# A two-block residual convolution network on one Trainium2 core: SBUF-to-SBUF transfers of the mixed stage sent by quarters, two for each unit of products

## The chip, the cores and the metric

The kernel runs on one core of one Trainium2 chip. The core has a matrix engine (TensorE; PE in the profile, its weight loads PEld), a vector engine (DVE), a scalar engine (ACT), GpSimd (POOL) and SyncE (SP), which here only issues transfers. Each engine works through its own instructions in order and waits on semaphores for the others. Every transfer that is issued from SP stands in SP's queue in program order: one that has to wait, or takes long to issue, holds up those behind it.

The metric is the device time of one execution in microseconds (us), lower is better. All data is float32.

## The reference

Two bottleneck blocks of a residual network, one after the other, on x of shape (64, 1024, 14, 14). Batch statistics are taken over all 64 images, so every normalization needs the whole convolution before it.

```python
def _bn(x, gamma, beta):
    mean = jnp.mean(x, axis=(0, 2, 3), keepdims=True)
    var = jnp.var(x, axis=(0, 2, 3), keepdims=True)
    ...
out = relu(_bn(_conv(x, w1, b1, 1, 0), g1, be1))     # 1x1, 1024 -> 256
out = relu(_bn(_conv(out, w2, b2, 1, 1), g2, be2))   # 3x3, 256 -> 256
out = _bn(_conv(out, w3, b3, 1, 0), g3, be3)         # 1x1, 256 -> 1024
out = softplus(residual_scale)[0] * out
out = relu(x + out)
```

## The kernel before

The 64 images are 32 tiles of two images, 392 pixels each (`T` = 32, `PX` = 392). Channels lie on the 128 partitions: 256 channels are two slots `s`, 1024 channels are eight slots `o`. The output of the second convolution of all images, `y_all`, stays on chip: 128 x 2 x 12544.

Block 0 runs as first convolution, second convolution, the **mixed stage** (`mixed`), and the **fused stage** (`fused`), which does the rest of block 0 together with the first convolution of block 1. Block 1 then has its own second convolution, a stage for statistics, and the final one.

**The mixed stage** needs the mean and variance of the third convolution over all images before that convolution can be normalized. It gets them in two ways at once:

- *The second half of the images* (tiles 16 to 31) is multiplied by w3 at once, and the raw result z is written out to be picked up later. Tile 16 goes first, in `first()` (L1522 to L1544 or so), as eight plain convolutions `conv3`, one for each output slot, with banks of the matrix engine's memory named cy, cx, cp, ay, ap, ax. Tiles 17 to 31 go through `direct_stream` (L605 and on): 60 **units**, four to a tile, each with two output slots and seven half-size products instead of eight (class `Direct`). A unit is cut into seven steps (0 to 6); the caller gets control after every step. Steps 0, 2, 3 and 4 are the products p1, p5, p2 and p6 of this unit, steps 1, 5 and 6 the products p7, p4 and p3 of the unit before. `after1` (ACT) copies bank cy to cx, on which p2 then adds; `after7` is L591 and `after3` is L597, both on DVE. Each unit writes its result to `kept[:, q]`, one of four slots, q = unit mod 4. The first write is that of p5 in step 2. When p3 of the unit is done, L599 sends the slot to z from SP's queue. The same slot is written again four units later, and that write has to wait until the transfer has landed.
- *The first half* (tiles 0 to 15, 6272 pixels) needs only the sums over pixels of y times y transposed (the gram matrix, `gram_products`). It is cut in five **pieces** (`MOVES`: four of 1280 pixels, one of 1152). Each piece is normalized on ACT (`norm_piece`, eight instructions of a quarter of the piece and one slot s), has a constant taken off on DVE (`less`, L1457; "centred"), is sent from `y_all` to a `home` by sixteen SBUF-to-SBUF transfers on SP's queue (`move`, L1493: four partition blocks i to four places j; i also picks a quarter of the pixels), and then transposed by DVE in chunks of 128 pixels, two at a time (`turn`, L1251). Two homes take turns: piece k needs the transposes of piece k - 2 to be done. Four chunks are a batch of gram products on the matrix engine; there are thirteen batches, at units 9, 12, ... 45 (`at`), fed by the generator `batches()`: the products of a batch at step 2, the transposes at step 3 of that unit and of the next.

The loop at the end of `mixed` lays all of this beside the units by hand: one normalization for each unit (`norms`, step 1), centrings at step 3, `moves = {9: 1, 17: 2, 25: 3, 33: 4}` (all sixteen transfers of piece 1 at unit 9, and so on). Piece 0 is normalized inside `first()`, two instructions behind each of the plain convolutions 3 to 6; its centring and its sixteen transfers follow `first()`. The order of matrix-engine, ACT and most other instructions is kept as it stands in the program (`keep_in_program_order`, `pinned`).

**The fused stage** reads z back in rows of 392 (tile p, slot o), eight for each of the tiles 16 to 31. A row is scaled and added to x, with DVE (L1828) for even o and with POOL (`by_pool`: L1814 multiplies, L1815 adds) for odd o. The POOL instructions of the first tile's four odd rows are put in front of the loop; for those rows the loop then only goes on with what follows. On POOL they stand ahead of the additions L537 and L542 of the stage's own products. ACT's relu behind L542 stands in ACT's order ahead of `au` (`after1` of `Conv1`), which the products `ay<-at,ws` of the matrix engine wait for.

Of the kernel before, what the change touches and what calls it, by code (L numbers as in the profile page):

```python
# [18 lines left out]
CS = C // P  # L19
MS = M // P  # L20
# [6 lines left out]
CH = 2  # L27
NZT = 6

Q = P // 2  # L30
# [8 lines left out]
NGRAM = KEPT * PX  # L39
MOVES = 5 * P * CH, 5 * P * CH, 5 * P * CH, 5 * P * CH, 9 * P  # L40
BATCH = 4
# [28 lines left out]
def bottlenecks(ctx: ExitStack, tc: tile.TileContext, x, w1s, w2s, w3s, pars, out):  # L70
# [6 lines left out]
    y_all = keep.tile([P, MS, NPX], FP, tag="y", name="y")  # L77
# [1363 lines left out]
    def mixed(psum, pool, one, x_right, x_left, aff, minus_c, w3, made_c, summed_c, summed_a, mv3, xs, coming_x):  # L1441
# [14 lines left out]
        def less(y, s, eng=nc.vector):  # L1456
            tc.keep_in_program_order(eng.tensor_scalar(y, y, minus_c[:, s : s + 1], None, ALU.add))  # L1457
# [3 lines left out]
        def norm_piece(k):  # L1461

            a, e = pieces[k]
            for s in range(MS):
                for i in range(4):
                    h = (e - a) // 4
                    norm(s, y_all[:, s, a + i * h : a + i * h + h], aff, act)
                    normed[k] += 1
                    yield

        def home(k):
            a, e = pieces[k]
            x = homes[k % 2][:, : MS * (e - a)].rearrange("p (s j f) -> p s j f", s=MS, j=4)
            return x, a, (e - a) // 4

        centered = collections.Counter()

        def center():

            k = next((k for k in range(len(pieces)) if centered[k] < MS * 2), None)  # L1480
            if k is not None and normed[k] >= 2 * centered[k] + 2:
                s, i = divmod(centered[k], 2)
                a, e = pieces[k]
                h = (e - a) // 4 * 2
                less(y_all[:, s, a + i * h : a + i * h + h if i == 0 else e], s)
                centered[k] += 1

        def move(k):
            assert centered[k] == MS * 2 and (k < 2 or k - 2 in turned)
            x, a, run = home(k)  # L1490
            for i, j in itertools.product(range(4), range(4)):
                tc.keep_in_program_order(
                    nc.sync.dma_start(  # L1493
                        out=x[32 * i : 32 * i + 32, :, j],
                        in_=y_all[32 * j : 32 * j + 32, :, a + i * run : a + i * run + run],
                    )
                )

        def blocks(t):
            return [[two(t, s)[:, i * H // 2 : (i + 1) * H // 2] for i in range(2)] for s in range(MS)]  # L1500
# [2 lines left out]
        ready = {}  # L1503
# [20 lines left out]
        def first():  # L1524


            t = KEPT
            norm(0, two(t, 0), aff, act)
            normed_less(two(t, 1), 1, nc.vector)
            less(two(t, 0), 0)  # L1530
            tags = "cy", "cy", "cx", "cp", "ay", "ay", "ap", "ax"
            for i, (q, row) in enumerate(itertools.product(range(CS // 2), range(2))):
                z, o = kept[:, q, row], q + row * CS // 2
                ps = conv3(psum, t, o, w3, tags[i])
                act(z, ps, AF.Copy)
                nc.vector.bn_stats(own[:, o, 0, :], ps)
                if row:
                    put(t, q)
                if i == 0:
                    for _ in itertools.chain(summed_c, prepare(t + 1), itertools.islice(coming[t + 2], MS)):  # L1540
                        pass
                if 2 < i < 7:
                    next(norms)
                    next(norms)  # L1544

        def put(t, q):
            to = zs[t - KEPT].rearrange("p (s f) -> p s f", s=CS)[:, q :: CS // 2, :]
# [11 lines left out]
        def chunks():  # L1559

            for k, (a, e) in enumerate(pieces):
                x, count = home(k)[0], (e - a) // P
                for i in range(0, count, CH):
                    zt = next(zts)
                    turn(zt, x, i, min(CH, count - i))
                    if i + CH >= count:
                        turned.add(k)
                    for c in range(min(CH, count - i)):
                        yield zt[:, c], (k, i + c)

        def batches():
            queue, total = chunks(), NGRAM // P
            bounds = [*range(0, total, BATCH), total]
            ready = [list(itertools.islice(queue, BATCH))]
            yield
            for a, e in zip(bounds, bounds[1:]):
                for i, (v, _) in zip(range(a, e), ready.pop()):
                    gram_products(upper, lower, v, i == 0, i == total - 1, True)
                yield
                ready.append([])  # L1580
                for _ in range(BATCH // CH):
                    ready[0].extend(itertools.islice(queue, CH))
                    yield

        norms = itertools.chain.from_iterable(norm_piece(k) for k in range(len(pieces)))
        coming = {t: prepare(t) for t in range(KEPT + 1, T)}
        first()
        both = psum.tile(512, "ap")
        upper, lower = both[:, : 3 * Q + 1], both[:, 3 * Q + 1 : 5 * Q + 3]
        zts, by, gs = gram_tiles(pool, NGRAM, 3)  # L1590
        for _ in range(2 * MS):
            center()
        move(0)
        tail, grams = None, iter(())
        moves = {9: 1, 17: 2, 25: 3, 33: 4}
        at = list(range(9, 48, 3))
        at_first, _ = beds((None, None))
        made, done = [], []

        def make(*tags):  # L1600
            for tag in tags:
# [12 lines left out]
        def finish():  # L1614
            aggregated(3)
            make("cy", "cp")

        pinned.append(True)
        for unit, step in direct_stream(units(), between, finish):
            t, q = KEPT + 1 + unit // 4, unit % 4  # L1620
            if step == 1 and unit > 0:
                next(norms, None)
            if step == 3 and unit == at[0] - 1:
                grams = batches()
                next(grams)
            if step == 2 and unit in at or step == 3 and (unit in at or unit - 1 in at):
                next(grams, None)
            if step == 3:
                if q < 2 and t + 1 < T:
                    next(coming[t + 1], None)  # L1630
                if len(moves) > len(done):
                    center()
                if unit in moves:
                    done.append(unit)
                    move(moves[unit])
                if unit in (20, 23, 26, 29):
                    next(summed_a)
                if unit in (44, 48):
                    coming_x()
                if 50 <= unit < 50 + AHEAD:  # L1640
                    bring(at_first[unit - 50], unit - 50)
                if unit == 57:
                    assert next(tail, "end") == "end"
                    for half in range(2):
                        to = gram_entry[:, :, 3 * half : 3 * half + 3]
                        nc.gpsimd.memset(to[:, :, 0], NGRAM / 2)
                        run(nc.vector.tensor_copy(to[:, :, 1], mv3[:, :, 0]))
                        run(nc.vector.tensor_scalar(to[:, :, 2], mv3[:, :, 1], NGRAM / 2, None, ALU.mult))
            if step == 5 and q == 1 and t + 1 < T:
                next(coming[t + 1], None)  # L1650
            if step == 5 and unit == 57:
                column_sums(pool, blocks(positions()[2]), n, eng=nc.gpsimd, to=ahead())
            if unit == 59 and step in (3, 5):
                aggregated(step // 4)
            if step == 6 and unit > at[-1] + 1 and (tail is None or unit < 57):
                if tail is None:
                    assert next(grams, "end") == "end"
                    tail = conv3_stats(
                        psum, pool, (upper, lower, by, gs), w3, mv3, ("ax", "ap", "ax", "ap"), homes[1], ("ax", "ax", "ap")
                    )  # L1660
                next(tail, None)
# [116 lines left out]
    def fused(psum, pool, one, right, coming, xs, raw, w1, w3, aff, par, stats, border, begun):  # L1778
# [26 lines left out]
        def kept_rows():  # L1805
# [8 lines left out]
                run(nc.gpsimd.tensor_scalar(z, z, scale[:, o : o + 1], None, ALU.mult))  # L1814
                run(nc.gpsimd.tensor_add(v, v, z))  # L1815

            for o in range(1, CS, 2):
                by_pool(*row(o, 1, o), o)
            for r, (p, o) in enumerate(itertools.product(range(1, T, 2), range(CS))):
                while r == len(at) and later:  # L1820
                    later.pop(0)()
                    yield
                v, z = row(r, p, o)
                if o % 2:
                    if p > 1:
                        by_pool(v, z, o)
                else:
                    run(nc.vector.scalar_tensor_tensor(v, z, scale[:, o : o + 1], v, ALU.mult, ALU.add))  # L1828
                for q in behind[r]:
                    bring(at[q], q)  # L1830
                later.append(partial(rest, v, p, o))
                if len(later) > 2:
                    later.pop(0)()
                yield
# [365 lines left out]
```

## Time and profile before

| | us |
|---|---|
| median of 3 runs | 1922.06 |
| lowest, highest | 1920.35, 1925.96 |
| the profiled execution, its own time | 1926.02 |
| its span | 1924.2 |
| its mean granted clock of TensorE | 0.995 |

The span is the time from the first to the last instruction in the trace of that one execution. A row of a timeline gives start, duration (both in us from the span's start), engine and line, what is written and read, how many instructions are merged in it, and in brackets how long the engine idled before it and what ended that. "SPq" is SP's queue; the duration there is that of the issue, not of the transfer. In a table of DMA issues the last number is the median time from issue to landing. A row of a table of windows gives the window, its length, the busy time of each engine with the number of its instructions, the granted clock of TensorE (1.00 is full speed), the mean busy share of the DMA engines and GB/s.

### The profile page before, as it was taken

How to read it: one execution, taken by the hardware profiler on the slowest of the kernel's cores; microseconds unless marked ns; L12 is line 12 of the kernel's file. 1: busy time of each engine (PE TensorE's matmuls, PEld its weight loads, DVE VectorE, ACT ScalarE, POOL GpSimd, SP SyncE). 2: the span in 40 equal slices, each digit the busy share in tenths (PEclk: the TensorE clock that was granted, in tenths of full speed). 3: DMA queues.
4: the chain of work that ended last, by engine and by line, in shares of the span. 5: the costliest groups of instructions: out<-in, count | busy, mean ns of one | idle time of the engine just before them, and what ended most of it. 6: DMA issues, size and time to landing. Idle time of an engine off the chain costs nothing. (4 is left out here: it accounts for less than half of the span.)

```text
span 1924.2 us, 28592 instructions
## 1 busy us (share of the span) xinstructions
PE 1889.5 (98%) x9778; PEld 1569.0 (82%) x9778; DVE 1573.1 (82%) x2464; ACT 1087.6 (57%) x2275; POOL 748.5 (39%) x764
## 2 busy tenths in 40 slices
PE   9999999999998999999999999999999999999999
PEld 5555557999996788889999999989999987555555
DVE  5787767999996666778878787789999987888886
ACT  2222214676775554465555555456777782666666
POOL 0111100211206535277676777602112041776665
PEclk9999999999999999999999999999999999999999
DMA  7777644887953535678787789648879457799997
GB/s 286 274 249 260 221 163 146 208 220 209 219 186 127 170 130 176 215 286 287 293 297 284 277 308 276 240 159 214 218 208 223 156 151 282 253 348 342 346 347 271
DMA packets 262370, 458.20 MB, mean 238 GB/s; under 512 B 59152, under 2 KB 228976, under 8 KB 249040
## 3 DMA queue, kind: packets, MB, share of 16 engines
q1 hardware_dynamic: 225248, 374.88, 58.2%
q0 software_dynamic: 31216, 28.81, 7.6%
q10 hardware_dynamic: 5760, 52.67, 6.8%
q8 instruction: 78, 1.28, 0.3%
q14 instruction: 68, 0.56, 0.1%
HBM read 289.44 MB, written 141.03 MB: 224 GB/s over the span
## 5 line engine op out<-in xcount | busy, mean ns | idle before, releaser
L332 ACT ACTIVATE x<-x,shift 128x392 f32<-128x392 f32 x452 | 260.0, 614 | 78.2 <-DVE x L514 31.4
L159 PE MATMUL columns<-v,ub 128*128 128x224 f32 (+1 forms) x1536 | 302.5, 338 | 1.3 <-ACT columns L332 0.8
L159 PEld LDWEIGHTS columns<-v,ub 128*128 128x128 f32 x1536 | 268.7, 188 | 7.5 <-ACT columns L332 1.5
L332 ACT ACTIVATE cu<-cy,scale 128x196 f32<-128x196 f32 (+1 forms) x360 | 175.5, 500 | 168.8 <-PE cy L159 161.2
L159 PE MATMUL ay<-at,ws 128*128 128x196 f32 (+1 forms) x768 | 193.2, 383 | 3.4 <-ACT au L332 2.1
L159 PEld LDWEIGHTS ay<-at,ws 128*128 128x128 f32 x768 | 136.3, 190 | 38.8 <-ACT au L332 2.4
L514 DVE SCALAR_TENSOR_TENSOR x<-cp,scale,x 128x196 f32<-128x196 f32 (+1 forms) x240 | 124.6, 519 | 46.7 <-PE cp L159 45.2
L641 POOL TENSOR_TENSOR x<-x,cu 128x392 f32<-128x392 f32 x120 | 125.5, 1047 | 73.2 <-DVE x L514 72.4
L332 ACT ACTIVATE au<-ay 128x196 f32<-128x196 f32 (+1 forms) x140 | 53.8, 384 | 173.1 <-PE ay L159 158.9
L159 PE MATMUL l<-diffs,ub 128*128 128x224 f32 (+1 forms) x768 | 149.6, 337 | 0.3 <-ACT sd L1921 0.3
L159 PE MATMUL m<-sums,ua 128*128 128x224 f32 (+1 forms) x752 | 146.0, 336 | 0.2 <-DVE sums L757 0.2
L159 PEld LDWEIGHTS l<-diffs,ub 128*128 128x128 f32 x768 | 134.6, 189 | 1.2 <-ACT sd L1921 0.6
L159 PEld LDWEIGHTS m<-sums,ua 128*128 128x128 f32 x752 | 131.4, 189 | 1.4 <-DVE sums L757 0.8
L159 PE MATMUL cx<-y,w 128*128 128x196 f32 (+1 forms) x396 | 126.1, 404 | 0.8 <-POOL y L1522 0.8
L537 POOL TENSOR_TENSOR x<-x,cu 128x196 f32<-128x196 f32 (+1 forms) x120 | 104.8, 873 | 48.6 <-ACT cu L332 27.8
L1055 POOL DMA_DIRECT2D y<-f x24 | 32.7, 1687 | 232.4 <-DVE f L975 232.4
L159 PE MATMUL cy<-y,w 128*128 128x196 f32 (+1 forms) x372 | 117.3, 403 | 0.7 <-DVE y L1457 0.7
L542 POOL TENSOR_TENSOR x<-x,cu 128x392 f32<-128x392 f32 x60 | 79.5, 1325 | 87.2 <-DVE x L514 83.0
L332 ACT ACTIVATE y<-y,shift,scale 128x1568 f32<-128x1568 f32 (+7 forms) x94 | 106.7, 1154 | 6.6 <-DVE shift L1953 6.5
L206 POOL DMA_DIRECT2D u<-y x48 | 26.0, 543 | 213.2 <-ACT y L332 212.4
L159 PE MATMUL cy<-ct,wt 128*128 128x196 f32 x384 | 96.4, 333 | 10.9 <-ACT cu L332 10.8
L936 ACT ACTIVATE columns<-m 128x448 f32<-128x448 f32 (+1 forms) x144 | 70.9, 492 | 58.9 <-PE m L159 54.0
(303 smaller groups left out, 4560.2 us busy)
## 6 DMA issues: line engine op xcount, KB each, us to landing
ub<-u SPq DMA_DIRECT2D x92, 768.0 KB, 5.5
x<-in_x SPq DMA_DIRECT2D x35, 1568.0 KB, 8.5
mid<-x ACTq DMA_DIRECT2D x32, 1568.0 KB, 8.1
x<-mid SPq DMA_DIRECT2D x32, 1568.0 KB, 8.7
out<-x SPq DMA_DIRECT2D x123, 392.0 KB, 7.0
x<-in_x SPq DMA_DIRECT2D x108, 392.0 KB, 7.8
z<-kept SPq DMA_DIRECT2D x64, 392.0 KB, 3.0
ua<-u SPq DMA_DIRECT2D x92, 256.0 KB, 3.1
```

What stands on the lines that cost most here:

```text
L159: tc.keep_in_program_order(nc.tensor.matmul(*args, **kw))
L206: nc.gpsimd.dma_start(out=us[b][i][:, s, o], in_=u)
L332: tc.keep_in_program_order(nc.scalar.activation(*args, **kw))
L514: run(nc.vector.scalar_tensor_tensor(v, bank, self.scale[:, o : o + 1], v, ALU.mult, ALU.add))
L537: run(nc.gpsimd.tensor_add(self.part(1, 1), self.part(1, 1), u3))
L542: run(nc.gpsimd.tensor_add(v, v, self.u12))
L641: nc.gpsimd.tensor_add(v, v, self.u12[:, i * self.n : (i + 1) * self.n])
L936: copy(v, m, AF.Copy)
L1055: nc.gpsimd.dma_start(out=out_rows[3][:, o], in_=fa[:, o, :full], accum_op=ALU.add)
```

## The change

In the mixed stage:

- A piece is normalized quarter by quarter (both slots s of a quarter, then the next), where it was slot by slot.
- A quarter is centred by two instructions of 320 (288 in the last piece) columns, one for each slot, where it was half a piece of one slot by one instruction. At units 2, 4, ... 32 one quarter each.
- The four transfers of a quarter can be sent as soon as that quarter is centred. Piece 0 is centred and sent quarter by quarter in `first()`, behind the plain convolutions 3 to 6. Pieces 1 to 4 are sent by two transfers a unit, in units 3 to 10, 13 to 20, 20 to 27 and 28 to 35.
- The first three steps of unit 0 are put in front of the last plain convolution of `first()`.
- The first two transposes, both at unit 8 before, are made at units 7 and 8.

In the fused stage the POOL instructions of the fourth odd row (row 7) go from in front of the loop to that row's place in the loop.

```diff
         def norm_piece(k):
             a, e = pieces[k]
-            for s in range(MS):
-                for i in range(4):
+            for i in range(4):
+                for s in range(MS):
                     h = (e - a) // 4
                     norm(s, y_all[:, s, a + i * h : a + i * h + h], aff, act)
...
-        def center():
-            k = next((k for k in range(len(pieces)) if centered[k] < MS * 2), None)
-            if k is not None and normed[k] >= 2 * centered[k] + 2:
-                s, i = divmod(centered[k], 2)
-                a, e = pieces[k]
-                h = (e - a) // 4 * 2
-                less(y_all[:, s, a + i * h : a + i * h + h if i == 0 else e], s)
-                centered[k] += 1
-
-        def move(k):
-            assert centered[k] == MS * 2 and (k < 2 or k - 2 in turned)
-            x, a, run = home(k)
-            for i, j in itertools.product(range(4), range(4)):
+        def center(k, i):
+            assert normed[k] >= MS * i + MS
+            for s in range(MS):
+                less(y_all[:, s, quarter(k, i)], s)
+
+        def move(k, i, places):
+            assert normed[k] >= MS * i + MS and (k < 2 or k - 2 in turned)
+            for j in places:
                 tc.keep_in_program_order(
                     nc.sync.dma_start(
-                        out=x[32 * i : 32 * i + 32, :, j],
-                        in_=y_all[32 * j : 32 * j + 32, :, a + i * run : a + i * run + run],
+                        out=home(k)[0][32 * i : 32 * i + 32, :, j], in_=y_all[32 * j : 32 * j + 32, :, quarter(k, i)]
                     )
                 )
...
             for i, (q, row) in enumerate(itertools.product(range(CS // 2), range(2))):
                 z, o = kept[:, q, row], q + row * CS // 2
+                if i == 7:
+                    for _ in itertools.islice(stream, 3):
+                        pass
                 ps = conv3(psum, t, o, w3, tags[i])
...
                 if 2 < i < 7:
                     next(norms)
                     next(norms)
+                    center(0, i - 3)
+                    move(0, i - 3, range(4))
...
-            ready = [list(itertools.islice(queue, BATCH))]
-            yield
+            ready = [[]]
+            for _ in range(BATCH // CH):
+                ready[0].extend(itertools.islice(queue, CH))
+                yield
...
-        for _ in range(2 * MS):
-            center()
-        move(0)
...
-        moves = {9: 1, 17: 2, 25: 3, 33: 4}
+        moves = {}
+        for k, begin in enumerate((3, 13, 20, 28), 1):
+            for i in range(8):
+                moves[begin + i] = moves.get(begin + i, ()) + ((k, i // 2, (i % 2 * 2, i % 2 * 2 + 1)),)
...
-            if step == 3 and unit == at[0] - 1:
-                grams = batches()
+            if step == 3 and at[0] - 3 < unit < at[0]:
+                grams = batches() if unit == at[0] - 2 else grams
                 next(grams)
...
-                if len(moves) > len(done):
-                    center()
-                if unit in moves:
-                    done.append(unit)
-                    move(moves[unit])
+                if 0 < unit <= 32 and unit % 2 == 0:
+                    center((unit - 1) // 8 + 1, (unit - 1) % 8 // 2)
+                for where in moves.get(unit, ()):
+                    move(*where)
...
-            for o in range(1, CS, 2):
+            for o in 1, 3, 5:
                 by_pool(*row(o, 1, o), o)
...
                 if o % 2:
-                    if p > 1:
+                    if p > 1 or o == CS - 1:
                         by_pool(v, z, o)
```

More of the change, by code (lines that the diff above doesn't have):

```diff
@@ L1474, in home, with quarter @@
             return x, a, (e - a) // 4
-        centered = collections.Counter()
-        def center():
-            k = next((k for k in range(len(pieces)) if centered[k] < MS * 2), None)
-            if k is not None and normed[k] >= 2 * centered[k] + 2:
-                s, i = divmod(centered[k], 2)
-                a, e = pieces[k]
-                h = (e - a) // 4 * 2
-                less(y_all[:, s, a + i * h : a + i * h + h if i == 0 else e], s)
-                centered[k] += 1
-        def move(k):
-            assert centered[k] == MS * 2 and (k < 2 or k - 2 in turned)
-            x, a, run = home(k)
-            for i, j in itertools.product(range(4), range(4)):
+        def quarter(k, i):
+            (a, e) = pieces[k]
+            h = (e - a) // 4
+            return slice(a + i * h, a + i * h + h)
+        moved = collections.Counter()
+        def center(k, i):
[5 more added lines that the diff above has]
+            for j in places:
                 tc.keep_in_program_order(
                     nc.sync.dma_start(
-                        out=x[32 * i : 32 * i + 32, :, j],
-                        in_=y_all[32 * j : 32 * j + 32, :, a + i * run : a + i * run + run],
+                        out=home(k)[0][32 * i : 32 * i + 32, :, j], in_=y_all[32 * j : 32 * j + 32, :, quarter(k, i)]
                     )
                 )
+                moved[k] += 1
         def blocks(t):
@@ L1566, in chunks @@
                     if i + CH >= count:
+                        assert moved[k] == 16
                         turned.add(k)
@@ L1586, in mixed @@
         coming = {t: prepare(t) for t in range(KEPT + 1, T)}
[L1587 to L1590, printed above, removed]
-        for _ in range(2 * MS):
-            center()
-        move(0)
         tail, grams = None, iter(())
-        moves = {9: 1, 17: 2, 25: 3, 33: 4}
+        moves = {}
+        for k, begin in enumerate((3, 13, 20, 28), 1):
+            for i in range(8):
+                moves[begin + i] = moves.get(begin + i, ()) + ((k, i // 2, (i % 2 * 2, i % 2 * 2 + 1)),)
         at = list(range(9, 48, 3))
         at_first, _ = beds((None, None))
-        made, done = [], []
+        made = []
         def make(*tags):
@@ L1616, in finish @@
             make("cy", "cp")
+        stream = direct_stream(units(), between, finish)
+        first()
+        both = psum.tile(512, "ap")
+        upper, lower = both[:, : 3 * Q + 1], both[:, 3 * Q + 1 : 5 * Q + 3]
+        zts, by, gs = gram_tiles(pool, NGRAM, 3)
         pinned.append(True)
-        for unit, step in direct_stream(units(), between, finish):
+        for unit, step in stream:
             t, q = KEPT + 1 + unit // 4, unit % 4
```

## The prediction

> **What bounds the kernel now.** I read the page first, then the waits of TensorE, then the timelines of PE, ACT, SP's queue, DVE and POOL through the mixed stage (588 to 812 us) and the first 30 us of the fused stage behind it, and the granted clock in short windows.
>
> ```profile
> PE 1889.5 (98%) x9778; PEld 1569.0 (82%) x9778; DVE 1573.1 (82%) x2464; ACT 1087.6 (57%) x2275; POOL 748.5 (39%) x764
> ```
>
> TensorE sets the time, so an edit pays only where PE stands still or runs at a lower clock. Nearly all of PE's stops in the mixed stage are these (start, duration, instruction; in brackets how long PE idled before it, and for whom):
>
> ```profile
> 599.72 0.57 PE L159 MATMUL cx<-y,w 128*128 128x196 f32 x2 [0.84 <-POOL y L1522]
> 603.08 0.57 PE L159 MATMUL cy<-ct,w 128*128 128x196 f32 x2 [0.44 <-DVE kept L591]
> 616.17 1.02 PE L159 MATMUL cy<-ct,wt 128*128 128x196 f32 x2 [4.62 <-ACT cu L332]
> 629.55 0.60 PE L159 MATMUL ay<-ct,wt 128*128 128x196 f32 x2 [0.78 <-DVE kept L597]
> 645.34 0.60 PE L159 MATMUL cy<-ct,wt 128*128 128x196 f32 x2 [0.97 <-ACT cu L332]
> 672.99 1.67 PE L159 MATMUL ay<-ct,wt 128*128 128x196 f32 x4 [2.72 <-ACT cu L332]
> 706.83 1.02 PE L159 MATMUL cy<-ct,wt 128*128 128x196 f32 x2 [3.29 <-ACT cu L332]
> 737.33 0.60 PE L159 MATMUL cy<-ct,wt 128*128 128x196 f32 x2 [1.88 <-ACT cu L332]
> ```
>
> The five that name ACT cu are 4.62 + 0.97 + 2.72 + 3.29 + 1.88 = 13.5 us. ACT's own timeline says what it waited for just before (two of the five):
>
> ```profile
> 615.33 0.33 ACT L332 ACTIVATE kept<-cp 128x196 f32<-128x196 f32 x1 [5.26 <-DMA z<-kept]
> ...
> 736.49 0.33 ACT L332 ACTIVATE kept<-cp 128x196 f32<-128x196 f32 x1 [5.61 <-DMA z<-kept]
> ```
>
> A unit writes one of four slots of kept; the slot must have been stored to z. SP's queue shows why a store is late:
>
> ```profile
> 601.88 10.40 SPq L1493 DMA_DIRECT2D home<-y  x16
> 612.40 17.67 SPq L599 DMA_DIRECT2D z<-kept  x8
> ```
>
> Sixteen transfers of one move hold SP for 10.4 us (0.65 each). The store behind them starts at 612.40 and frees its slot 2.93 us later (615.33). Five moves, five stops. The clock adds to them; the windows begin where PE resumes (length, busy time of PE, PEld, DVE, ACT, POOL, granted clock, DMA share, GB/s):
>
> ```profile
> 616.20:624.00 7.80, 7.80 (x32) 7.76 (x32) 3.72 (x9) 4.66 (x15) 0.72 (x1) 0.67 0.37 136
> 673.00:681.00 8.00, 8.00 (x47) 6.57 (x48) 1.61 (x4) 2.27 (x7) 2.99 (x3) 0.60 0.23 83
> 706.80:712.80 6.00, 5.97 (x35) 5.56 (x37) 3.77 (x9) 3.36 (x10) 2.00 (x2) 0.73 0.39 143
> 737.30:743.30 6.00, 5.97 (x36) 5.48 (x38) 4.36 (x11) 3.95 (x13) 2.82 (x3) 1.00 0.36 136
> 831.50:840.00 8.50, 8.45 (x41) 8.45 (x42) 3.87 (x8) 4.16 (x10) 4.28 (x4) 0.80 0.95 342
> ```
>
> Length times missing clock is 7.8 x 0.33 = 2.6, 8 x 0.40 = 3.2, 6 x 0.27 = 1.6, 0 and 8.5 x 0.20 = 1.7 us.
>
> **The change part by part.**
>
> *Moves 1 to 4, two transfers a unit.* The count of transfers stays. A unit now asks SP for one store (0.51) and two transfers (1.3): 1.8 us, 3.1 in unit 20, where pieces 2 and 3 both send. A unit lasts 2.4 us, and a store has room, by these rows (ACT's writes of units 7 and 8, SP's store of unit 6) and the median landing:
>
> ```profile
> 624.47 0.32 ACT L332 ACTIVATE kept<-ay 128x196 f32<-128x196 f32 x1
> 626.86 0.32 ACT L332 ACTIVATE kept<-cp 128x196 f32<-128x196 f32 x1
> ...
> 626.13 0.51 SPq L599 DMA_DIRECT2D z<-kept  x1
> ...
> z<-kept SPq DMA_DIRECT2D x64, 392.0 KB, 3.0
> home<-y SPq DMA_DIRECT2D x64, 80.0 KB, 2.1
> ```
>
> Unit 6's slot is written again by unit 10, two units after 626.86, at 631.6; the store of 626.13 lands at 629.1. That is 2.5 us of slack, and two transfers in front cost 1.3. So stops two to five go: 0.97 + 2.72 + 3.29 + 1.88 = **-8.9**, and with them the clock, 3.2 + 1.6 = **-4.8**. Queued behind a waiting transfer on SP are only later stores; each transfer waits for a centring issued a unit before, and for the home's last transposes, also a unit before. Without that lead the store behind would wait for DVE. The centrings become two of 320 columns for one of 640 in the same units; twenty more DVE instructions go into DVE's gaps, so 0; bound +1. The gaps are in the row of the whole stage (length, busy time of PE, PEld, DVE, ACT, POOL):
>
> ```profile
> 588.00:812.00 224.00, 207.75 (x1318) 180.39 (x1317) 146.46 (x327) 120.08 (x351) 106.78 (x122) 0.96 0.50 164
> ```
>
> What could be late next is the transpose, which wants a whole piece landed. The last pair of a piece now goes one unit ahead of the first transpose of pieces 2 and 4 (units 20 and 21, 35 and 36):
>
> ```profile
> 627.32 1.29 DVE L1251 STREAM_TRANSPOSE zt<-home 128x512 f32<-128x512 f32 x2
> ...
> 651.65 0.69 DVE L1251 STREAM_TRANSPOSE zt<-home 128x512 f32<-128x512 f32 x1
> 656.57 0.69 DVE L1251 STREAM_TRANSPOSE zt<-home 128x512 f32<-128x512 f32 x1
> ```
>
> Behind a store the pair lands after 0.51 + 0.65 + 2.1 = 3.3 us, a unit later is 2.4: DVE may wait some 1 us, twice. It falls where PE does a batch of gram products (the two transposes of a batch stand 4.9 us apart, 2.5 more than a unit), so I charge 0, bound +3. The first two transposes (627.32, 1.29 us in one go) are now split over units 7 and 8, which takes away the 0.78 at 629.55: **-0.8**.
>
> *Move 0 and the first products.* Its quarters are centred and sent inside first(). DVE's four centrings then no longer stand ahead of L591, and the 0.44 at 603.08 goes. Rows of DVE, then ACT:
>
> ```profile
> 594.34 0.55 DVE L1536 BATCH_NORM_STATS2 stats<-cp 128x6 f32<-128x392 f32 x1
> ...
> 599.88 2.78 DVE L1457 TENSOR_SCALAR y<-y,minus_c 128x640 f32<-128x640 f32 x4
> ...
> 597.78 1.19 ACT L332 ACTIVATE y<-y,shift,scale 128x320 f32<-128x320 f32 x2
> 599.25 0.32 ACT L332 ACTIVATE cx<-cy 128x196 f32<-128x196 f32 x1
> 607.58 0.32 ACT L332 ACTIVATE kept<-ay 128x196 f32<-128x196 f32 x1
> ```
>
> ACT works without a gap here, so PE's products for unit 0 in front of the last plain convolution help only by the one copy (0.48) that cx<-cy overtakes: PE's 0.84 shrinks to about 0.4. Together **-0.9** (0 if it is POOL, as the row says, that PE waits for).
>
> The first stop does not go wholly. The first centring pair (695 ns for 640 columns, so about 0.35 for each of 320) follows the 594.34 row and ends at 595.6. From there SP has sixteen transfers and one store, 10.4 + 0.6, so the last store of first(), emitted behind them, goes at 606.6 and lands at 609.6. Unit 3 writes that slot (kept<-ay at 607.58, less 0.9 = 606.7). ACT waits 2.9, PE 0.6 less as before (5.26 against 4.62): 2.2 in place of 4.62, **-2.4**. The bounds are 0 and 4.6. Whether the clock drops after 2.2 is open between rows: 1.88 kept it, 2.72 lost 3.2. I take half of the 2.6: **-1.3**.
> The Trainium skill, "TensorE: Matmul & The Clock Gate", section "Why this matters for your kernels", asks that PE never idle more than about 3 us between bursts; by that rule the 2.2 us would cost no clock and the sum would be 1.3 better. The 2.72-us stop followed by 0.60 speaks against taking it as sharp.
>
> *Fused stage.* Row 7's pair on POOL goes from the four pairs ahead of the loop to its place as row 7.
>
> ```profile
> 816.34 1.28 POOL L1814 TENSOR_SCALAR y<-y,scale 128x392 f32<-128x392 f32 x1 [29.38 <-DVE scale L2143]
> ...
> 826.06 0.60 POOL L537 TENSOR_TENSOR x<-x,cu 128x196 f32<-128x196 f32 x1
> 826.62 1.34 POOL L542 TENSOR_TENSOR x<-x,cu 128x392 f32<-128x392 f32 x1
> ...
> 827.99 1.65 ACT L332 ACTIVATE x<-x,shift 128x392 f32<-128x392 f32 x3 [1.97 <-POOL x L542]
> ...
> 831.55 0.93 PE L159 MATMUL ay<-at,ws 128*128 128x196 f32 x4 [2.07 <-ACT au L332]
> ...
> 828.82 0.97 DVE L440 TENSOR_TENSOR at<-at,x 128x784 f32<-128x784 f32 x1
> ```
>
> Four pairs take 9.7 us, 2.4 each. L542 ends 2.3 sooner, ACT starts its 1.97 sooner, and PE could resume at 829.6; its operand at (828.82 + 0.97) allows 829.85: 1.7 off the 2.07. The clock behind it is 1.7. I take **-3.0**, between -3.4 and +2.4 (the pair stands ahead of an L537 or L542 that PE waits for).
>
> Sum: 8.9 + 4.8 + 0.8 + 0.9 + 2.4 + 1.3 + 3.0 = 22.1. The profiled execution took 1926.0 (span 1924.2, 1.8 around it), so 1903.9 for it. That execution is 4.0 over the median of the runs shown (1922.06), which spread over 5.6; against the median I forecast 1900.0.
>
> **The rivals.**
>
> *Half paid.* The last store of first() waits as long as now and the POOL pair only changes place: 22.1 - 2.4 - 1.3 - 3.0 = 15.4, and 1.6 of the clock stays: -13.8, 1908. For it: all sixteen transfers of move 0 are still ahead of that store. Against it: they start 6 us sooner (595.6, not 601.88).
>
> *All paid.* Unit 3 reaches its slot only after 609, with no stop and no clock lost there: 22.1 + 2.2 + 1.3 = 25.6, 1896. For it: ACT is without a gap in first() and in order, and could carry the first units late. Against it: with the same work it wrote that slot at 607.58.
>
> *Slower.* Now 31 units (3 to 10, 13 to 35) each have transfers on SP ahead of their store. If a pair waits there, for the centring of its quarter on DVE or the norm behind it on ACT, the stores inherit it in every unit. It decides once a store is 2.5 us late; at 3.2 the loss is 31 x 0.7 = 22 us and the gain is gone; at 3.6 it is 31 x 1.1 = 34, and the time 1934. Against it: the centring has a unit's lead.
> The Trainium skill, "DMA: Bandwidth & Descriptors", section "Queues, rings and completion order", says that each DMA engine takes descriptors in the order of a queue's ring, so a store behind transfers also waits for their data. The store at 612.40 stood behind sixteen and landed in 2.93 against a median of 3.0; by that row it adds nothing.
>
> *Nothing.* The stage turns out to be held by DVE (busy 146 of its 224 us) once SP is free, and the stops reappear as waits for DVE kept: -4 to 0, 1920.
>
> **How the numbers follow.** Forecast 0.66, half paid 0.14, all paid 0.09, nothing 0.06, slower 0.05. About 0.3% (5.8 us) can be told from no change. Faster: 0.66 + 0.14 + 0.09 = 0.89; same 0.06; slower 0.05. Low end: all paid less 2 for the spread of runs, 1894. High end: half paid with the front's 0.9 and 2 for the spread, 1911.
>
> **What would show it.** Right: SP's queue with pairs between single stores; no ACT kept waiting for z<-kept after about 612; one such wait near 607 of 2 to 3 us; PE clock 1.00 from 650 to 750; PE's wait for au in the fused stage under 0.5. Wrong: ACT waits for z spread over many units, DVE zt waiting for home with PE idle in the same unit, or PE waits for DVE kept in place of ACT cu.

## The result, and the profile after

| | before | after |
|---|---|---|
| median, us | 1922.06 (5 runs, 1917.66 to 1925.96) | 1907.68 (5 runs, 1906.14 to 1909.31) |
| profiled execution, us | 1926.02 | 1907.06 |
| its span, us | 1924.2 | 1905.3 |
| its mean granted clock | 0.995 | 0.999 |

The ratio is 0.9925 with a 95% interval of 0.9908 to 0.9943: 14.4 us faster (11 to 18). The forecast was 22.1 us faster, 1900.0, and its range of 1894 to 1911 holds the result.

First, where the 18.9 us between the two spans are. ACT takes one square root at the start of the mixed stage, one at its end, which is the start of the fused stage, and one at the end of the fused stage; these are rows of ACT's timeline, of before and then of after.

```profile
584.52 0.29 ACT L1921 ACTIVATE sd<-mv,eps 128x2 f32<-128x2 f32 x1 [4.81 <-DVE mv L1905]
814.34 0.30 ACT L1921 ACTIVATE sd<-mv,eps 128x8 f32<-128x8 f32 x1 [2.46 <-DVE mv L1607]
1264.40 0.29 ACT L1921 ACTIVATE sd<-mv,eps 128x1 f32<-128x1 f32 x1 [0.91 <-DVE mv L1905]
```

```profile
584.00 0.29 ACT L1928 ACTIVATE sd<-mv,eps 128x2 f32<-128x2 f32 x1 [4.80 <-DVE mv L1912]
797.85 0.30 ACT L1928 ACTIVATE sd<-mv,eps 128x8 f32<-128x8 f32 x1 [2.45 <-DVE mv L1610]
1244.37 0.29 ACT L1928 ACTIVATE sd<-mv,eps 128x1 f32<-128x1 f32 x1 [0.91 <-DVE mv L1912]
```

| stretch, us | before | after | difference |
|---|---|---|---|
| up to the mixed stage | 584.52 | 584.00 | -0.5 |
| mixed stage | 229.82 | 213.85 | -16.0 |
| fused stage | 450.06 | 446.52 | -3.5 |
| the rest, to the end of the span | 659.80 | 660.93 | +1.1 |

The +1.1 is not work of the change. The same stop of PE, 1.95 us, is at 1269.81 before and at 1249.77 after, and in the 7.8 us behind it the clock was 1.00 in the one trace and 0.78 in the other.

PE's timeline of the mixed stage after, all stops from 590 to 700 us (one of 0.74 stands at 586.90, as one of 0.73 did before; one more of 0.34 follows at 752, as there was one at 768 before):

```profile
598.82 0.57 PE L159 MATMUL cx<-y,w 128*128 128x196 f32 x2 [0.46 <-ACT cx L332]
610.69 0.60 PE L159 MATMUL cy<-ct,wt 128*128 128x196 f32 x2 [3.01 <-ACT cu L332]
623.94 0.60 PE L159 MATMUL ay<-ct,wt 128*128 128x196 f32 x2 [0.70 <-DVE kept L597]
631.64 0.60 PE L159 MATMUL ay<-ct,wt 128*128 128x196 f32 x2 [0.18 <-DVE kept L597]
652.06 0.60 PE L159 MATMUL ay<-ct,wt 128*128 128x196 f32 x2 [0.47 <-DVE kept L597]
665.56 0.60 PE L159 MATMUL ay<-ct,wt 128*128 128x196 f32 x2 [1.16 <-DVE kept L597]
673.27 0.60 PE L159 MATMUL ay<-ct,wt 128*128 128x196 f32 x2 [0.18 <-DVE kept L597]
685.79 0.60 PE L159 MATMUL ay<-ct,wt 128*128 128x196 f32 x2 [0.16 <-DVE kept L597]
694.02 0.60 PE L159 MATMUL ay<-ct,wt 128*128 128x196 f32 x2 [0.66 <-DVE kept L597]
```

The eight stops shown before were 15.5 us, with the 0.34 at 768 15.9; these nine are 7.0, with the 0.34 7.3. That is 8.6 us less standing still. The other 7.4 of the stage's 16.0 is the clock: 2.6 + 3.2 + 1.6 us were lost behind the stops before, and the windows of after have 1.00 from 600 to 760 us. Four of the five stops for a store are gone, one of 3.0 is left, and seven short waits for L597 on DVE stand where there was one, the 0.78 at 629.55.

SP's queue after, at the place of the stop that is left, with the row of ACT's wait behind it:

```profile
595.66 5.28 SPq L1492 DMA_DIRECT2D home<-y  x8
601.05 0.57 SPq L1552 DMA_DIRECT2D z<-kept  x1
601.71 5.11 SPq L1492 DMA_DIRECT2D home<-y  x8
606.92 0.57 SPq L1552 DMA_DIRECT2D z<-kept  x1
607.60 1.24 SPq L599 DMA_DIRECT2D z<-kept  x2
...
609.86 0.33 ACT L332 ACTIVATE kept<-ay 128x196 f32<-128x196 f32 x1 [3.75 <-DMA z<-kept]
...
619.24 1.26 SPq L1492 DMA_DIRECT2D home<-y  x2
620.62 0.57 SPq L599 DMA_DIRECT2D z<-kept  x1
```

The last store of first() goes at 606.92, behind sixteen transfers, and its slot is free at 609.86. From then on pairs stand between single stores, as in the last two rows.

### The profile page after: what moved, and what is told of

The parts are those of the page before. It is cut to its first block, busy times and chain, and to the rows that moved or that the text cites. A ratio compares the mean times of both kernels' runs of the same rounds, so it can differ in the third digit from the quotient of the medians.

```text
span 1905.3 us, 28617 instructions
## 1 busy us (share of the span) xinstructions
PE 1881.1 (99%) x9778; PEld 1560.8 (82%) x9778; DVE 1576.5 (83%) x2484; ACT 1088.6 (57%) x2275; POOL 749.4 (39%) x764
## 5 line engine op out<-in xcount | busy, mean ns | idle before, releaser
L206 POOL DMA_DIRECT2D u<-y x48 | 26.0, 544 | 212.9 <-ACT y L332 212.2
L1821 POOL TENSOR_SCALAR y<-y,scale 128x392 f32<-128x392 f32 x57 | 92.6, 1624 | 30.1 <-DVE scale L2150 29.4
```

What stands on the lines that cost most here:

```text
L206: nc.gpsimd.dma_start(out=us[b][i][:, s, o], in_=u)
```

## The experiments

Nine kernels. Their medians stand beside runs of the kernel before on the same chip (1921.5 to 1924.7 in the three jobs). The changed kernel's 1907.68 comes from a job of its own, with 1922.06 before; where a median is compared with it below, that is across jobs, and the traces carry more.

| kernel | median (lowest to highest), us | ratio to before, 95% interval |
|---|---|---|
| before, once more | 1922.86 (1918.60 to 1927.49) | 1.0004, 0.9995 to 1.0013 |
| pairs for pieces 1 to 4 only | 1910.69 (1910.20 to 1911.04) | 0.9935, 0.9921 to 0.9950 |
| POOL row only | 1921.33 (1917.03 to 1925.94) | 0.9992, 0.9982 to 1.0002 |
| after, without the front products | 1907.85 (1906.96 to 1909.62) | 0.9923, 0.9910 to 0.9935 |
| after, without the POOL row | 1908.73 (1906.68 to 1912.30) | 0.9914, 0.9900 to 0.9927 |
| after, piece 0 spread | 1903.99 (1903.67 to 1905.05) | 0.9901, 0.9883 to 0.9918 |
| after, centring spread | 1905.76 (1904.27 to 1907.39) | 0.9909, 0.9891 to 0.9928 |
| after, both spread | 1901.62 (1900.58 to 1903.42) | 0.9886, 0.9865 to 0.9907 |
| after, eight transfers at a time | 1912.44 (1911.99 to 1913.16) | 0.9944, 0.9927 to 0.9962 |

**The kernel before, once more.**

> The kernel before once more, unchanged, for the spread of its own time and the granted clock of each execution. Theory A (what the clock loses after the stops of the mixed stage differs from execution to execution): the times lie between 1917 and 1926 as before and go with the clock, the shorter ones at 0.997 or more, the longer at 0.995, and the trace has other lost windows than the 2.6, 3.2 and 1.6 us of the first trace, while the five stops for z keep their sum of 13.5 us within 0.5. Theory B (the spread comes from elsewhere): times do not go with the clock.

Of 35 executions of the kernel before in one job (twelve of this kernel, 23 beside it), sorted by their granted clock:

| clock | executions | median us | range us |
|---|---|---|---|
| 0.994 | 1 | 1926.6 | |
| 0.995 | 8 | 1924.9 | 1924.3 to 1927.5 |
| 0.996 | 12 | 1922.7 | 1921.4 to 1923.5 |
| 0.997 | 8 | 1921.2 | 1920.7 to 1922.1 |
| 0.998 | 4 | 1920.2 | 1919.9 to 1920.4 |
| 0.999 | 2 | 1918.9 | 1918.6 to 1919.3 |

The time goes with the clock, some 1.5 us for each 0.001 (7.7 us from 0.999 to 0.994): theory A. The stops are the same from trace to trace: here 4.62, 1.42, 2.73, 3.25 and 1.50, again 13.5 in sum. What differs is what the clock does behind them. The trace quoted in the prediction was one at 0.995; the median execution, at 0.996 to 0.997, is 4 us shorter and so, by estimate, has lost some 5 of its 9.1 us. One part of theory A did not come: in the mixed stage this trace has much the same low windows as the first (0.62, 0.60 and 0.73 behind the same stops). Only in the fused stage is it 1.00 where the first lost 1.7; the plain proof that the same stop may cost nothing is in the next-but-one kernel.

**Pairs alone.** Of the change only pieces 1 to 4, with the centring by quarters. Nothing is sent in first(); piece 0 is centred and sent in one go behind it. The first transposes, the front products and the POOL row are as before.

```diff
+        for i in range(4):
+            center(0, i)
+        for i in range(4):
+            move(0, i, range(4))
         pinned.append(True)
```

> Of the change only the pairs of transfers of pieces 1 to 4 and their centring by quarters; move 0 behind first() in one go, the first transposes at unit 8, the front products and the POOL row as before. Theory (a store waits behind sixteen transfers): no ACT wait for z after about 620, the first one stays at 5.3 us and PE's first stop at 4.6 with its loss of clock; PE waits for DVE kept of 3 to 4 us in all. Mixed stage 9 to 12 us shorter in the trace than the 229.8 of before; time 1911 to 1915. Rival (DMA bandwidth, not the order on SP, makes the stores late): waits for z stay at more than 5 us behind unit 8.

The four later waits for z are gone (one of 0.63 stands at 767, far behind the moves, as one of 0.50 does with the change), and PE waits for L597 4.1 us in all. Mixed stage 215.7 us, 14.1 shorter than before (9 to 12 expected); the median is 0.3 below what was expected. The miss is the first stop. It did not stay at 4.62 but became these two (PE's timeline, then SP's queue):

```profile
603.87 0.57 PE L159 MATMUL cy<-ct,w 128*128 128x196 f32 x2 [2.07 <-DVE kept L591]
614.35 0.60 PE L159 MATMUL cy<-ct,wt 128*128 128x196 f32 x2 [0.41 <-ACT cu L332]
...
600.00 10.49 SPq L1492 DMA_DIRECT2D home<-y  x16
```

Eight centrings in a row on DVE hold L591 for 2.07, and SP begins its sixteen transfers at 600.00, as soon as the first quarter is centred and with the last store of first() already gone. So sending piece 0 out of first() in the middle, the other part of the change for that piece, gains nothing in stops: 2.07 + 0.41 without it, 3.01 with it, and over the whole stage PE stands as long with the one as with the other. The stage is 1.9 us longer here than with the change because of the clock: 0.78 in the 7.8 us behind the 2.07 (1.7 us), where it was 1.00 behind the 3.01.

**The POOL row alone.** The kernel before with

```diff
-            for o in range(1, CS, 2):
+            for o in 1, 3, 5:
                 by_pool(*row(o, 1, o), o)
...
-                    if p > 1:
+                    if p > 1 or o == CS - 1:
```

> Of the change only the POOL row 7 in the fused stage. Theory: fused stage 3 to 3.6 us shorter (450.1 us between the two square roots before), PE's wait for au 2.1 down to under 1 and the clock behind it at 0.95 or more; time 1917 to 1919.5. Rival (the stage is held by its z reads and x loads anyway): the stage stays within 1 us, 1921 to 1923.

Fused stage 446.8 us, against 450.1 and 448.3 in the two traces of before, and PE's wait for au is gone: the theory's mechanism. The median, 0.6 us below before with an interval from -3.5 to +0.4, does not resolve it and lies in the rival's range, not the theory's: the ten executions spread over 8.9 us with the clock. This trace holds the proof for the clock. PE's timeline at the stops of 672.99 and 706.83 of the first trace:

```profile
671.19 0.93 PE L159 MATMUL ay<-ct,wt 128*128 128x196 f32 x4 [2.71 <-ACT cu L332]
701.97 0.60 PE L159 MATMUL cy<-ct,wt 128*128 128x196 f32 x2 [3.23 <-ACT cu L332]
```

and the windows behind them, as in the prediction's table:

```profile
671.20:679.20 8.00, 7.95 (x63) 6.94 (x63) 4.55 (x11) 4.67 (x15) 3.01 (x3) 1.00 0.36 135
701.90:707.90 6.00, 5.93 (x52) 5.28 (x53) 4.42 (x10) 3.40 (x11) 2.05 (x2) 1.00 0.50 185
```

The mixed stage is that of before, instruction for instruction, and the stops are as long, 2.71 and 3.23. But the clock stays at 1.00 (0.60 and 0.73 there), and PE begins 63 products in 8 us where it began 47. The mixed stage took 223.7 us in place of 229.8.

**Without the front products.** The changed kernel with

```diff
-                if i == 7:
-                    for _ in itertools.islice(stream, 3):
-                        pass
```

> The changed kernel with the first three steps of unit 0 behind the last plain convolution again. Theory (ACT, busy without a gap there, sets when cx is ready): PE's stop ahead of the first product on cx grows from 0.46 to about 0.84, the later first stop for z shrinks by as much, so the time stays within 0.5 us of the changed kernel: 1907 to 1908.5. Rival (the front products are worth their 0.9): 1908.5 to 1909.5.

PE's stop ahead of cx is 0.84 again, the first stop for z 2.78 in place of 3.01, the median within 0.2 us of the changed kernel. As the theory has it, of the 0.38 that PE gains in front it gives 0.23 back at the next wait. The mixed stage of this trace is 215.5 us, 1.7 longer than with the change: behind the 2.78 the clock was 0.78 for 7.8 us.

**Without the POOL row.** The changed kernel with `range(1, CS, 2)` in front of the fused loop and `if p > 1` in it again.

> The changed kernel with row 7's POOL pair in front of the fused loop again. Theory (the pair stands ahead of L542, ACT waits for that, and TensorE for ACT's au): TensorE's wait for au is 2.07 us again where the changed kernel has none, the fused stage is 3 to 3.6 us longer in the trace than the 446.5 of the changed kernel, and the time is 1910 to 1912. Rival (the edit is worth only what the kernel before showed with it alone, 0.6 us): 1907.5 to 1908.5.

```profile
819.65 0.93 PE L159 MATMUL ay<-at,ws 128*128 128x196 f32 x4 [2.06 <-ACT au L332]
```

That row of PE's timeline is back, and in the changed kernel there is none. The fused stage is 448.4 us, 1.9 longer than the 446.5 of the changed kernel, less than expected: in this trace the clock did not fall behind the 2.06. The median is 1.05 us above that of the changed kernel, with ranges that overlap, and 15.9 below its own runs of before, where the change is 14.4 below; between the theory's 2.3 to 4.3 and the rival's 0.8 at most the times don't decide. What is shown is the stop. The mixed stage is that of the change, instruction for instruction, with a first stop of 3.03, and yet 215.5 us long: behind that stop the clock was 0.78 for 7.8 us (its row is in the last section).

**Piece 0 spread.** Half of piece 0's transfers stay in first(), the other half goes to units 0 to 3:

```diff
-                    move(0, i - 3, range(4))
+                    n = i - 3
+                    move(0, n // 2, (n % 2 * 2, n % 2 * 2 + 1))
...
+                if unit < 4:
+                    move(0, 2 + unit // 2, (unit % 2 * 2, unit % 2 * 2 + 1))
                 for where in moves.get(unit, ()):
```

> The changed kernel, but only two of piece 0's transfers behind each of the plain convolutions 3 to 6 (quarters 0 and 1), the other eight two at a time in units 0 to 3. Theory (the last store of first() stands behind sixteen transfers): that store is issued at about 601.5 in place of 606.9, ACT's wait of 3.75 and PE's stop of 3.01 go; mixed stage 3 us shorter in the trace than the 213.9 of the changed kernel; time 1904 to 1905.5. Rival (the slots are late from landing, not from the queue): the wait stays above 2 us.

SP's queue, and ACT's write of unit 3:

```profile
599.43 2.51 SPq L1492 DMA_DIRECT2D home<-y  x4
602.04 0.57 SPq L1553 DMA_DIRECT2D z<-kept  x1
602.70 2.51 SPq L1492 DMA_DIRECT2D home<-y  x4
...
606.38 0.33 ACT L332 ACTIVATE kept<-ay 128x196 f32<-128x196 f32 x1
```

The last store of first() goes at 602.04, the slot is written at 606.38 without a wait. PE's 3.01 is gone, the mixed stage is 211.6 us (2.2 shorter and not 3, for 0.7 us of waits for DVE are new), and the time is 3.7 us below the changed kernel. The two traces are 3.1 us apart, and 1.3 of that lies behind the fused stage, where the clock stayed at 1.00 behind the 1.95-us stop; it is not of this edit. In all four executions the clock was 1.000. The order on SP, not the landing, made that store late.

**Centring spread.** One slot of a quarter at each unit, where both were at the even ones:

```diff
-                if 0 < unit <= 32 and unit % 2 == 0:
-                    center((unit - 1) // 8 + 1, (unit - 1) % 8 // 2)
+                if 0 < unit <= 32:
+                    center((unit - 1) // 8 + 1, (unit - 1) % 8 // 2, [(unit - 1) % 2])
```

> The changed kernel with the two centring instructions of a quarter in two units, one slot at each unit from 1 to 32, in place of both at the even ones. Theory (two centrings, 0.5 us each on average, stand ahead of L597 on DVE): PE's waits for DVE kept L597 fall from 3.8 us in eight to under 2; time 1905 to 1907. Rival (the transposes, or DVE's work in sum, make L597 late): they stay at 3.3 us or more, 1907 to 1908.5.

PE's waits for L597 are 1.1 us in four (3.8 in eight with the change), the median 1.9 below the changed kernel. The mixed stage of the trace, 212.9 us, is only 0.9 shorter, because behind the first stop, here 3.15, the clock was 0.78 for 7.8 us (1.7 us). The 32 centrings keep DVE as busy as with the change, 14.8 us against 14.6, so it is their place ahead of L597 and not DVE's work in sum: the theory and not the rival. What the pair does is seen in DVE's timeline of the changed kernel in unit 20, ahead of the longest wait, 1.16 at 665.56 (there a sum of weights, L140, stands behind the pair as well; with the pair split, 0.42 of this wait is left):

```profile
662.96 1.28 DVE L1457 TENSOR_SCALAR y<-y,minus_c 128x320 f32<-128x320 f32 x2
664.15 1.08 DVE L140 TENSOR_TENSOR ws<-w 128x512 f32<-128x512 f32 x1
665.16 0.35 DVE L597 TENSOR_TENSOR kept<-ay,cu 128x196 f32<-128x196 f32 x1
```

and its price in the groups by form, first of before, then of after (count, busy us, mean ns):

```profile
L1457 DVE TENSOR_SCALAR y<-y,minus_c 128x640 f32<-128x640 f32 x16 | 10.4, 666 | 0.0
```

```profile
L1457 DVE TENSOR_SCALAR y<-y,minus_c 128x320 f32<-128x320 f32 x32 | 14.6, 497 | 0.0
```

Half the columns cost 497 ns, not 333. The two of a pair overlap a little; by the busy time a pair is 14.6 / 16 = 0.91 us where one instruction was 10.4 / 16 = 0.65.

**Both spread.** The last two edits together.

> Both of the two before. If they are independent, the mixed stage is shorter by the sum, 4.5 to 5 us; time 1902 to 1904.

Mixed stage 209.3 us, 4.6 shorter than with the change, and 1901.62, 0.4 below the range. PE's stops from 590 us to the end of the stage are 7.3 us with the change, 5.0 with piece 0 spread, 4.8 with the centring spread and 2.6 with both. So the edits save 2.3, 2.6 and together 4.7: in stops they are independent. (The lengths of the stage don't show it, 2.2 and 0.9 against 4.6, for the trace with the centring spread lost 1.7 to the clock.) This version beats both kernels and is 6.1 us below the changed one.

**Eight at a time.** Two quarters of a piece, each whole, at two units four apart:

```diff
-            for i in range(8):
-                moves[begin + i] = moves.get(begin + i, ()) + ((k, i // 2, (i % 2 * 2, i % 2 * 2 + 1)),)
+            for i in range(4):
+                at_unit = begin + i // 2 * 4 + 3
+                moves[at_unit] = moves.get(at_unit, ()) + ((k, i, range(4)),)
```

> The changed kernel with pieces 1 to 4 sent eight transfers at a time, at two units four apart. Eight hold SP for 5.2 us; a unit is 2.4, so the next store is late by some 2.8 at most, against a slack of 2.5. Theory (a store's lateness counts only beyond its slack): ACT's waits for z in pieces 1 to 4 are 0.5 us or less each, PE's below 0.2, and the time stays within 1 us of the changed kernel, 1907 to 1909. Rival (what SP is held for costs in proportion): half of the old stops two to five, 4 us, 1911 or more.

4.8 us slower than the change, as the rival has it in size, but not for its reason. ACT's waits for z while pieces 1 to 4 are sent are one of 1.15 (0.5 expected), which stops PE nowhere. The mixed stage is 217.3 us, 3.4 longer than with the change, with the clock at 1.00 behind the first stop in both; the other 1.5 us between the two traces lies outside the stage. What costs is the other end, in DVE's and PE's timelines:

```profile
670.78 0.71 DVE L1251 STREAM_TRANSPOSE zt<-home 128x512 f32<-128x512 f32 x1 [2.96 <-DMA home<-y]
694.74 0.71 DVE L1251 STREAM_TRANSPOSE zt<-home 128x512 f32<-128x512 f32 x1 [1.43 <-DMA home<-y]
724.63 0.71 DVE L1251 STREAM_TRANSPOSE zt<-home 128x512 f32<-128x512 f32 x1 [4.54 <-DMA home<-y]
...
696.64 0.60 PE L159 MATMUL ay<-ct,wt 128*128 128x196 f32 x2 [1.97 <-DVE kept L597]
726.60 0.57 PE L159 MATMUL cy<-ct,w 128*128 128x196 f32 x2 [1.53 <-DVE kept L591]
```

The last eight transfers of a piece land after its first transpose is due, DVE stands, and what is behind it, L591 or L597, keeps PE waiting. With pairs the same place costs DVE 0.26 once. Of PE's two waits 0.66 was there with the change; the other 2.8 us are most of the 3.4. So eight in front of a store stopped PE nowhere here; eight in front of a transpose, one unit ahead, did.

## Why the prediction was right, and where it was too large

- *What is late and why* was right. Stores wait on SP behind a move's transfers; with pairs the stops two to five are gone (8.9 forecast, 8.9 measured), and the spread of piece 0 shows the same for the one that was left.
- *The first stop* was foreseen with its place and time: store at 606.6 forecast, 606.92 measured, landing 609.6 and 609.86. PE stood 3.01, not 2.2: ACT's wait was 3.75, not 2.9, so the term is -1.6 and not -2.4. The clock did not drop behind it in this trace (1.3 better than charged), and that is luck: in three of the five traces with such a first stop it did, by 1.7 us, so half of 2.6 was a fair charge for the mean.
- *Centring in DVE's gaps, 0, bound +1* is the step that failed. DVE has gaps in the sum, but at step 3 the pair stands right ahead of L597, for which PE waits. Where the prediction prices such an instruction, "about 0.35 for each of 320" from the four in a row, it cost 0.5 each, and the waits came to 3.5 us more than the 0.34 that stays, well over the bound (of these 0.70 is the wait that splitting the first transposes was to remove and did not: 0.78 before). Centring spread shows the cause.
- *The transpose wanting a whole piece, 0* held with pairs (0.26 of DVE, no stop of PE); with eights it is the thing that costs, so the bound of +3 was no idle one.
- *The front products* are worth nothing of their own: 0.17 us without them.
- *The fused stage* took the whole stop of 2.07 away (1.7 forecast; 828.82 + 0.97 is 829.79 and not 829.85, so 1.8 by the prediction's own rows). The trace's 3.5 for the stage holds 1.6 to 1.7 of clock; 1.9 is what the pair of traces without that loss shows.
- *From the trace to the median* is the other step that failed. The sum was made against the execution of 1926.0, whose lost clock of 9.1 us it contains, and was then taken off the median of 1922.06 unchanged. That median execution had lost some 4 us less, so it had as much less to win.

Against the profiled execution the forecast of 22.1 stands beside 19.0. Off by term: front and first stop 0.9, first transposes 0.7, waits for L597 2.8, against 1.3 of clock and 0.5 in the fused stage the other way, and 0.6 outside these stages. Of the 4.6 from there to the 14.4 of the medians, 4.0 is that the profiled execution of before lay so far above its median, which goes with the clock, and 0.6 that the one of after lay below its own. Of the rivals, "half paid" (1908) comes closest in time, but not in mechanism: the fused edit did what it should. Its 1908 also set the upper end of the range, so that the range holds 1907.68 owes much to it; the forecast's own 1900.0 is 7.7 us off. "Nothing" named waits for DVE kept in place of waits for ACT cu; that is what took 3.5 us back, and it was among the signs of being wrong.

By the Trainium skill's rule on gaps, "TensorE: Matmul & The Clock Gate", section "Why this matters for your kernels", no gap under about 3 us should have cost clock. Here 3.01 with the change and 3.23 with the POOL row alone cost none, while 2.72 before cost 3.2 us and 2.07 with the pairs alone 1.7. The same page, section "What's actually happening", calls the activity window free-running. That fits the same stop with two outcomes, though no run here shows the window itself; a price per stop then has to be a mean over executions.

## What to carry to other kernels

When a stall comes from a queue that is held, compute the hold against the slack of each thing behind it, and then look at what the other end of the moved transfers is due for: here a store forgave eight transfers in front, a transpose one unit later did not. Before work is cut into halves on an engine that is "not the bottleneck", find which instruction stands behind it and who waits for that; its average load does not tell. And take a clock loss from several executions, not from one trace, before it is subtracted from a median.

## What the runs showed of the hardware

The clock behind a stop is not fixed by its length. One stop of 2.7 us, same instructions, was followed by a clock of 0.60 in one execution and 1.00 in another. The first stop of the mixed stage shows it again. These are the windows behind it with the change and without the POOL row, two kernels whose mixed stages are the same:

```profile
610.70:618.50 7.80, 7.80 (x46) 7.45 (x46) 6.28 (x16) 6.62 (x21) 6.77 (x8) 1.00 0.78 251
```

```profile
613.60:621.40 7.80, 7.76 (x36) 7.60 (x37) 4.96 (x12) 5.42 (x17) 6.56 (x8) 0.78 0.65 204
```

| kernel | first long stop, us | clock in the 7.8 us behind it |
|---|---|---|
| the change | 3.01 | 1.00 |
| eight transfers at a time | 3.02 | 1.00 |
| without the POOL row | 3.03 | 0.78 |
| centring spread | 3.15 | 0.78 |
| without the front products | 2.78 | 0.78 |
| pairs for pieces 1 to 4 only | 2.07 | 0.78 |

0.78 over 7.8 us is 1.7 us. What decides between the two values no run here shows. In the 35 executions of the kernel before, whose stops are the same in its two traces but for half a microsecond, most of the spread of 8.9 us goes with the clock.

A DVE tensor_scalar of 320 columns takes 0.34 to 0.38 us when POOL rests and from 0.34 up to 0.76 beside it. Two single ones of the kernel with the centring spread, from the timelines of DVE and POOL:

```profile
646.31 0.34 DVE L1457 TENSOR_SCALAR y<-y,minus_c 128x320 f32<-128x320 f32 x1
...
635.93 0.60 POOL L479 TENSOR_TENSOR ct<-y 128x196 f32<-128x196 f32 x1
636.14 0.57 DVE L1457 TENSOR_SCALAR y<-y,minus_c 128x320 f32<-128x320 f32 x1
```

Part of what halving costs is there without POOL too: a pair at rest keeps DVE busy 0.64 us (at 630.68 with the change), one of 640 columns 0.54 (at 622.40 before). That is 0.10 of the 0.26 us by which a pair is dearer in the mean.

The Trainium skill, "SBUF — State Buffer", section "Who interferes with whom", says that a tensor_scalar can run in a mode that uses both of DVE's port pairs, one of them shared with POOL, and that whoever issues first then holds the shared pair for its whole instruction. By that rule each start can wait for the other engine once. More instructions then mean more such waits, which agrees with the rest of the 0.26 us; it was read from the overlaps and not tried by itself, and no run here shows the mode.
